# First linear map by 128-row blocks, the last four blocks' h kept on chip, y stored in 512-byte pieces

## The chip, the core and the metric

The kernel runs on one core of a Trainium2 chip. The metric is device time in microseconds (us), the median over runs of the same program. A profiled execution is one more run, with the hardware profiler on. Engines: PE is TensorE's matmul part and PEld its weight load, DVE is VectorE, ACT ScalarE, POOL GpSimd, SP SyncE, which here only issues DMAs. Each engine works through its own instructions in a fixed order; semaphores hold it where it needs another's result.

## The reference, cut to what matters

```python
# x: (8, 2048, 256); A: (2048, 2048), sparse, symmetric pattern; W1: (512, 256); W2: (256, 512)
A_norm = A + eye(n)
deg = sum(A_norm, axis=0) + sum(A_norm, axis=1) - diagonal(A_norm)
dinv = rsqrt(deg)
A_hat = A_norm * dinv[:, None] * dinv[None, :]
agg = einsum('nm,bmd->bnd', A_hat, x)
h = relu(batchnorm(agg.reshape(-1, 256) @ W1.T + b1))    # statistics over all 8 x 2048 rows
out = batchnorm(h @ W2.T + b2)
x1 = layernorm(x + out)
# then masked multi-head attention on x1 (4 heads of 64, mask where A is 0), residual and layernorm
```

Everything is float32. The change concerns the lines from `agg` to the product with `W2`. Both batch norms need all rows before the first normalised value exists, so they cut the program into stages.

## The kernel before

The 2048 rows are 16 blocks of 128, named t. Rows of all 8 batches stand side by side: a scaled x row is 8 x 256 = 2048 values, 8 KB, so one 128-row tile is 1 MB. Sixteen such tiles of chip memory, the "slots", are handed out by a small free list (class `Slot`), and every part of the first layer takes its large tiles from them.

*Dense stage* (lines 377 to 467). The adjacency rows are read and searched for their nonzeros; x is read in 1 KB rows, scaled by `dinv` and stored to `xs_d`; blocks 0 and 1, the dense ones, are summed over all of x with matmuls (L454).

*Sparse stage* (lines 469 to 628). For blocks 2 to 15 the neighbours of a row are listed, and a "tile" is one neighbour per row: GpSimd gathers 128 rows of `xs_d` by index (`gather`, L524, 1 MB) and beforehand the 128 adjacency values that go with them (L311). There are 116 tiles. A tile is added either by TensorE, as four 128x512 products with a one-hot or diagonal weight tile (L606), or by VectorE, as a multiply-add over 2048 columns (L593 for the first, L597 for the others). Blocks 2 and 3 have 14 and 11 tiles, of which 3 each are VectorE's; blocks 4 to 15 have 10 down to 6, of which 1 to 3 are TensorE's. VectorE also still searches the last adjacency rows (L219, L223, L226) during blocks 2 and 3. When a block's tiles are done, `add_rows` joins both sums (L355, four pieces, VectorE).

The gathers run ahead of their use. `gather_ahead` issues up to 8 tiles ahead, as long as more than `keep` slots are free; `keep` is 2, or 6 while the four turned tiles of the current four-block set have not yet been taken.

*First linear map.* `turn_rows` transposes a finished block (four transposes, one PSUM bank, one ACT copy L373; four times per block). The copies fill slots `agt[c, g]`: c is the set of four blocks (512 rows), g a pair of batches. So the four slots of a set are full when the fourth block is turned. Then `linear_steps(c, g)` computes h for two batches by 512 rows: for each 128 of the 512 outputs, two matmuls of 128x512 (four records in the trace, L489), one ACT copy with bias (L493), one `bn_stats` on VectorE (L476, issued one unit later). Call that a unit; there are 128. After four units an h tile of 1 MB is stored to `h_d` by SP (L496).

The order is written out by hand (`manual_schedule`). A list `work` holds generators; after each tile `do_work` takes one unit or one transposed quarter of it (two after a VectorE tile). Transposes go to the front of the list, linear units to its end: those of a set enter after its fourth block. What is left at the end of the tile loop is emitted in a row.

*Last loop and second linear map* (lines 636 to 792). The last four of the 32 h tiles are not stored. Their 16 units (L747) are interleaved with the finish of the first batch norm (`bn1.root`, `bn1.affine`) and with the ReLUs (L676) of the first two pairs of tiles. The other 28 tiles are read back (`read_h`), two per pair, up to 7 pairs ahead. For each pair `second_linear` makes the product with W2 by seven products of half size (Strassen's scheme; the differences of tiles are formed on GpSimd, L694, the products on TensorE, L699) and stores two y tiles of 512 KB to `y_d` (L729, L737), in rows of 4 KB. Then the second batch norm is finished and attention begins, whose first step loads y by batch and set of 512 rows (L870).

Of the kernel before, what the change touches and what calls it, by code (L numbers as in the profile page):

```python
# [8 lines left out]
F32 = mybir.dt.float32  # L9
# [4 lines left out]
AF = mybir.ActivationFunctionType  # L14
# [24 lines left out]
def tile_gcn_then_masked_attention(  # L39
# [15 lines left out]
    nc = tc.nc  # L55
    ENG = mybir.EngineType
    PSUM = bass.MemoryType.PSUM
    P = 128
# [276 lines left out]
    ps_a = None  # L335
    agr, agt = {}, {}

# [20 lines left out]

    def as_agt(s):
        return s.t.rearrange("p (d b n) -> p d b n", d=ND, b=2)  # L360

    def turn_rows(t, g, psum):

        c, i = divmod(t, TPC)
        if not i:
            agt[c, g] = Slot()
        ps = psum.tile([P, ND, 2, P], F32, name="ph")
        for d in range(ND):
            for b in range(2):
                r0 = (2 * g + b) * D + d * P  # L370
                nc.tensor.transpose(ps[:, d, b, :], agr[t].t[:, r0 : r0 + P], ident)
        dst = as_agt(agt[c, g])[:, :, :, i * P : (i + 1) * P]
        nc.scalar.copy(dst, ps)  # L373
        if g == B // 2 - 1:
            agr.pop(t).done()
# [93 lines left out]
    with tc.tile_pool(name="l0", bufs=1, side="right", reuse_waits="tile") as lp, tc.tile_pool(  # L469
        name="psh", bufs=4, space=PSUM  # L470
    ) as psh, tc.manual_schedule(engines=ALL4):
        last_stats = []

        def flush_stats():
            while last_stats:
                nc.vector.bn_stats(*last_stats.pop())  # L476

        def linear_steps(c, g):

            s = agt[c, g]  # L480
            v = as_agt(s)
            for b in range(2):
                k = (2 * g + b) * NCH + c
                h = lp.tile([P, NH, CH], F32, name="h", bufs=2)
                for f in range(NH):
                    flush_stats()
                    ph = psh.tile([P, CH], F32, name="ph")
                    for d in range(ND):
                        nc.tensor.matmul(  # L489
                            ph, w1s[:, d, f * P : (f + 1) * P], v[:, d, b, :],  # L490
                            start=(d == 0), stop=(d == ND - 1),
                        )
                    nc.scalar.activation(h[:, f, :], ph, AF.Identity, bias=b1s[:, f : f + 1])  # L493
                    last_stats.append((st1[:, f, k, :], h[:, f, :]))
                    if f == NH - 1:
                        nc.sync.dma_start(h_d[k], h)  # L496
                        if b:
                            s.done()
                    yield
# [29 lines left out]
        def gather_ahead(n):  # L529
            t = tiles[min(n, len(tiles) - 1)][0]  # L530
            keep = 2 if (t // TPC, B // 2 - 1) in agt else 2 + B // 2
            while gathered[0] < min(n + 8, len(tiles)) and (
                len(free) > keep or gathered[0] <= n
            ):
                gather(gathered[0])
                gathered[0] += 1
# [22 lines left out]
        def turn_steps(t):  # L559
            for g in range(B // 2):  # L560
                turn_rows(t, g, psh)
                yield

        for _ in turn_steps(0):
            pass
        work += [turn_steps(t) for t in range(1, DENSE)]
        gather_ahead(0)
# [3 lines left out]
        for n in range(len(tiles)):  # L571
# [40 lines left out]
            if n + 1 == first[t + 1]:  # L612
                add_rows(t, pa)
                do_work(2)
                work.insert(0, turn_steps(t))
                if t % TPC == TPC - 1 and t < NT - 1:
                    work += [linear_steps(t // TPC, g) for g in range(B // 2)]
            else:
                do_work(1 + mine)
        assert not making  # L620
        for f in work:
            for _ in f:
                pass
        for g in range(2):
            for _ in linear_steps(NCH - 1, g):
                pass
        flush_stats()
    right.close()
    middle.close()

    last4 = [b * NCH + NCH - 1 for b in range(B // 2, B)]
    others = [i for i in range(NALL) if i not in last4]
    pairs = [last4[:2], last4[2:]]
    pairs += [others[i : i + 2] for i in range(0, len(others), 2)]

    with tc.tile_pool(name="l1", bufs=1, side="right", reuse_waits="tile") as lp, tc.tile_pool(
        name="psa", bufs=4, space=PSUM
    ) as psa, tc.tile_pool(name="psh", bufs=4, space=PSUM) as psh, tc.manual_schedule(engines=ALL4):
        hin = {}

        def read_h(n):
            hin[n] = [Slot() for _ in range(2)]
            if n > 1:
                for r in range(2):
                    nc.sync.dma_start(hin[n][r].t, h_d[pairs[n][r]].rearrange("p f n -> p (f n)"))

        def h_tile(n, r):
            return hin[n][r].t.rearrange("p (f n) -> p f n", f=NH)

        w2s = [lp.tile([P, 2, O], F32, name=f"w2s{j}") for j in range(2)]  # L650
        w2f = [lp.tile([P, 2, P], F32, name=f"w2f{j}") for j in range(4)]
        for j in range(2):
            nc.sync.dma_start(
                w2s[j], w2t[j * 2 * P : (j + 1) * 2 * P].rearrange("(c p) f -> p c f", p=P)
            )
        for n in range(7):
            read_h(n)
# [45 lines left out]

        def first_product(n):
            Y[n] = [lp.tile([P, NO, CH], F32, name=f"y{n % 2}{r}") for r in range(2)]
            p1 = product2(W[0, 0], h_half(n, 0, 0))
            nc.scalar.copy(Y[n][0][:, 1, :], p1)
# [7 lines left out]
        def plus(dst, p, u, o):  # L715
            nc.vector.scalar_tensor_tensor(
                dst, p, b2s[:, o : o + 1], u, op0=ALU.add, op1=ALU.add
            )

        def second_linear(n):  # L720
            (c11, c21), (c12, c22) = ([Y[n][r][:, o, :] for o in range(NO)] for r in range(2))
# [6 lines left out]
            stats2(n, 1, 0)  # L728
            nc.sync.dma_start(y_d[pairs[n][0]], Y[n][0])  # L729
            if n not in P5:  # L730
# [5 lines left out]
            stats2(n, 0, 1)  # L736
            nc.sync.dma_start(y_d[pairs[n][1]], Y[n][1])  # L737
            for s in hin.pop(n):
# [3 lines left out]
        for f in range(NH):  # L742
            for n in range(B // 2):
                ph = psh.tile([P, CH], F32, name="ph")
                v = as_agt(agt[NCH - 1, B // 4 + n // 2])
                for d in range(ND):
                    nc.tensor.matmul(  # L747
                        ph, w1s[:, d, f * P : (f + 1) * P], v[:, d, n % 2, :],
                        start=(d == 0), stop=(d == ND - 1),
                    )  # L750
                h = h_tile(n // 2, n % 2)[:, f, :]
                nc.scalar.activation(h, ph, AF.Identity, bias=b1s[:, f : f + 1])
                nc.vector.bn_stats(st1[:, f, last4[n], :], h)
                if n == 0 and f:
                    bn1.affine(f - 1)
            bn1.root(f)
            if f:
                relu(0, f - 1)
                relu(1, f - 1)
            if f == 2:  # L760
                form(0, 1)
                form(1, 1)
        for g in range(B // 4, B // 2):
            agt[NCH - 1, g].done()
        bn1.affine(NH - 1)
        first_product(0)
        fifth_product(0, psh, "ph")
        first_product(1)
        fifth_product(1, psh, "ph")
# [4 lines left out]
        for n in range(len(pairs)):  # L774
            if n > 1:
                first_product(n)
            if 1 <= n < len(pairs) - 1:
# [4 lines left out]
            second_linear(n)  # L782
            if n + 7 < len(pairs):
                read_h(n + 7)

# [913 lines left out]
```

## Time and profile before

| | us |
|---|---|
| median of 3 runs | 2288.48 |
| lowest, highest | 2283.89, 2298.30 |
| profiled execution | 2305.59 |
| its span, first to last instruction | 2303.9 |

| stage, us from the span's start | length | PE busy | DVE busy | DMA share |
|---|---|---|---|---|
| dense, 0 to 185.4 | 185.4 | 149.4 | 141.5 | 0.80, then 0.84 |
| sparse and first linear, 185.4 to 583.5 | 398.1 | 360.1 | 360.9 | 0.90 |
| rest of the first linear, 583.5 to 663.2 | 79.7 | 76.8 | 37.2 | 0.53 |
| second linear, 663.2 to 845.5 | 182.3 | 180.5 | 118.4 | 0.52 |
| attention, 845.5 to 2303.9 | 1458.4 | 1233.4 | 1171.2 | 0.85 |

A stage's busy time is the time in which an engine had an instruction running; the difference to the stage's length is waiting. The DMA share is the mean busy share of the core's 16 DMA engines. The costliest groups around the change, from the page (line, engine, operation, out<-in, shape, count | busy us, mean ns of one | idle us just before them and what ended it):

```profile
L489 PE MATMUL ph<-e,w1s 128*128 128x512 f32 x448 | 197.4, 593 | 0.0
L524 POOL DMA_INDIRECT e<-xs_d,idx x116 | 152.9, 1318 | 138.9 <-DMA xs_d<-xt 66.6
L606 PE MATMUL pa<-e,wt 128*128 128x512 f32 x352 | 166.4, 621 | 14.6 <-DMA e<-xs_d,idx 11.2
L493 ACT ACTIVATE h<-ph,b1s 128x512 f32<-128x512 f32 x112 | 77.0, 687 | 179.9 <-PE ph L489 166.1
```

Matmuls are pipelined, so the 593 ns of one are longer than the distance from one to the next.

### The profile page before, as it was taken

Reading aid. Unit: us, or ns where it says so; the run is one execution under the profiler, and the core shown is the slowest. Engines: PE = TensorE matmul, PEld = TensorE weight load, DVE = VectorE, ACT = ScalarE, POOL = GpSimd, SP = SyncE. Lnnn points to the kernel's source line nnn. Section 1 sums busy time; section 2 is a strip of 40 time slices with the busy share of each in tenths; the row PEclk is TensorE's granted clock in tenths of the full one; section 3 lists DMA queues with packets and bytes.
Section 4 is the critical chain, followed back from the end, with each engine's and each line's share of the span. In section 5 each row is a group of like instructions: output and inputs, shape, how many; then the busy total and the mean of one; then the engine's idle time right before and its main releaser. Section 6 shows DMA issues by size and latency. Waiting matters only on the chain.

```text
span 2303.9 us, 27757 instructions
## 1 busy us (share of the span) xinstructions
PE 2000.2 (87%) x7720; PEld 1296.2 (56%) x7720; DVE 1829.2 (79%) x3461; ACT 1306.1 (57%) x3896; POOL 1443.2 (63%) x1443
## 2 busy tenths in 40 slices
PE   5899897898999979789889898989889999778774
PEld 1444443444444436566767766766667777556663
DVE  6888998798466652168799988889978999978896
ACT  6221132233355536556667776767767777678785
POOL 2505778884067741246667776667766777867784
PEclk7899998999999989989999999999999999889996
DMA  7888998899466445658889988789898899999994
GB/s 310 294 290 321 349 375 335 347 392 388 184 258 263 159 147 202 227 202 317 319 295 370 339 319 347 296 303 365 325 341 322 325 347 333 339 338 320 341 335 154
DMA packets 232628, 698.67 MB, mean 303 GB/s; under 512 B 24976, under 2 KB 91280, under 8 KB 206352
## 3 DMA queue, kind: packets, MB, share of 16 engines
q0 software_dynamic: 109248, 442.68, 52.1%
q1 hardware_dynamic: 120912, 237.34, 28.1%
q10 hardware_dynamic: 2304, 16.78, 1.8%
q8 instruction: 64, 1.05, 0.2%
q14 instruction: 100, 0.82, 0.1%
HBM read 565.91 MB, written 130.81 MB: 302 GB/s over the span
## 4 chain that ended last, share of the span: by engine, by line
PE 50%; DVE 23%; issue 7%; DMA 7%; ACT 5%; POOL 5%; another core or an unknown queue 1%; SPq 0%; DVEq 0%; ACTq 0%; POOLq 0%
PE po L1252 9%; PE pm L977 9%; PE pa L699 8%; PE ph L489 6%; DVE pr L1210 6%; PE pa L454 5%; DVE wv L1241 3%; DVE s L1212 3%; PE pa L606 3%; ACT wv L1236 2%; POOL kg L1192 2%; PE pm L1026 2%; PE po L1045 2%; DMA e<-in_adj_dram 2%; DMA e<-xs_d,idx 2%
## 5 line engine op out<-in xcount | busy, mean ns | idle before, releaser
L1192 POOL DMA_INDIRECT kg<-kv_d,idx x528 | 567.4, 1075 | 166.5 <-issue 102.9
L1252 PE MATMUL po<-wv,ident 128*128 128x260 f32 x1472 | 435.7, 407 | 96.5 <-DVE z L1066 85.6
L1236 ACT ACTIVATE wv<-kg,pw 128x65 f32<-128x65 f32 x1896 | 477.8, 338 | 21.3 <-issue 10.5
L1212 DVE TENSOR_REDUCE s<-pr 128x8 f32<-128x512 f32 x528 | 362.3, 686 | 34.4
L1252 PEld LDWEIGHTS po<-wv,ident 128*128 128x128 f32 x1472 | 278.5, 202 | 170.4 <-issue 107.9
L977 PE MATMUL pm<-wq,x1t 128*128 128x512 f32 (+1 forms) x1024 | 366.6, 489 | 1.0 <-ACT x1t L922 0.6
L1221 ACT ACTIVATE pw<-s,padb 128x8 f32<-128x8 f32 x528 | 156.6, 300 | 209.9 <-DVE s L1212 156.1
L1210 DVE TENSOR_TENSOR pr<-qb,kg 128x512 f32<-128x512 f32 x368 | 257.3, 699 | 5.0 <-DMA kg<-kv_d,idx 2.7
L1241 DVE TENSOR_TENSOR wv<-kg,pw 128x520 f32<-128x520 f32 x291 | 211.3, 726 | 58.7 <-PE po L1252 18.4
L977 PEld LDWEIGHTS pm<-wq,x1t 128*128 128x128 f32 x1024 | 193.8, 192 | 95.8 <-issue 74.1
L524 POOL DMA_INDIRECT e<-xs_d,idx x116 | 152.9, 1318 | 138.9 <-DMA xs_d<-xt 66.6
L1252 PE MATMUL po<-wv,oh 128*128 128x260 f32 x640 | 207.8, 415 | 0.3 <-DVE oh L1227 0.3
L489 PE MATMUL ph<-e,w1s 128*128 128x512 f32 x448 | 197.4, 593 | 0.0
L1198 POOL DMA_INDIRECT qg<-q_d,idxq x160 | 164.5, 1028 | 48.8 <-issue 47.8
L311 POOL DMA_INDIRECT av<-in_adj_dram,fidx x116 | 158.8, 1369 | 45.7 <-issue 32.3
L1026 PE MATMUL pm<-q,kt 128*128 128x256 f32 x512 | 141.9, 401 | 45.8 <-ACT kt L1014 19.1
L606 PE MATMUL pa<-e,wt 128*128 128x512 f32 x352 | 166.4, 621 | 14.6 <-DMA e<-xs_d,idx 11.2
L493 ACT ACTIVATE h<-ph,b1s 128x512 f32<-128x512 f32 x112 | 77.0, 687 | 179.9 <-PE ph L489 166.1
L1045 PEld LDWEIGHTS po<-kvr,p 128*128 128x128 f32 x1024 | 142.5, 203 | 22.9 <-ACT p L1034 11.4
L1073 POOL TENSOR_TENSOR x<-z,x 128x256 f32<-128x256 f32 x126 | 112.7, 896 | 57.1 <-DVE z L1066 52.5
L1045 PE MATMUL po<-kvr,p 128*128 128x65 f32 x1024 | 137.4, 280 | 11.5 <-ACT p L1034 8.9
L1026 PEld LDWEIGHTS pm<-q,kt 128*128 128x128 f32 x512 | 98.6, 199 | 84.3 <-ACT kt L1014 27.2
(192 smaller groups left out, 3399.0 us busy)
## 6 DMA issues: line engine op xcount, KB each, us to landing
kv_d<-kvr SPq DMA_DIRECT2D x32, 1032.0 KB
h_d<-h SPq DMA_DIRECT2D x28, 1024.0 KB
e<-h_d SPq DMA_DIRECT2D x28, 1024.0 KB
e<-in_adj_dram SPq DMA_DIRECT2D x16, 1024.0 KB
xt<-in_x_dram SPq DMA_DIRECT2D x16, 1024.0 KB
xs_d<-xt ACTq DMA_DIRECT2D x16, 1024.0 KB
y_d<-y SPq DMA_DIRECT2D x32, 512.0 KB
yt<-y_d SPq DMA_DIRECT2D x32, 512.0 KB
```

Source lines behind the costliest of these rows:

```text
L489: nc.tensor.matmul(ph, w1s[:, d, f * P : (f + 1) * P], v[:, d, b, :], start=(d == 0), stop=(d == ND - 1),)
L606: nc.tensor.matmul(pa[c], w, xg[n].t[:, c * CH : (c + 1) * CH], start=(k == 0), stop=(k == count - 1),)
L699: nc.tensor.matmul(py, w[:, f, :], t[:, f, :], start=(f == 0), stop=(f == 1))
L977: nc.tensor.matmul(pm, x1t[b, c][:, d, i * P : (i + 1) * P], rhs(d), start=(d == 0), stop=(d == ND - 1),)
L1026: nc.tensor.matmul(pm[:, hp].rearrange("p r q -> p (r q)"), k[:, hp, :], q0[b][:, hp].rearrange("p r q -> p (r q)"), start=False, stop=Tru ...
L1045: nc.tensor.matmul(po0[b][:, h, :], p[:, h, :], heads(kvr[b, c][:, i, D:])[:, h, :], start=(j == 0 and h == 0), stop=(j == NT - 1), skip_g ...
L1192: nc.gpsimd.indirect_dma_start(out=kg[n].rearrange("p b e -> p (b e)"), out_offset=None, in_=kv_d[p][:], in_offset=bass.IndirectOffsetOnAx ...
L1210: nc.vector.tensor_mul(pr, q, kg[n][:, :, :D])
L1212: nc.vector.tensor_reduce(s.rearrange("p b h -> p (b h)"), pr.rearrange("p b (h e) -> p (b h) e", e=HD), AX.X, ALU.add,)
L1236: nc.scalar.activation(wv[n][:, b, hs], k[:, b, D:][:, hs], AF.Copy, scale=w[:, b, h : h + 1],)
L1241: nc.vector.tensor_mul(wv[n].rearrange("p b (h e) -> p b h e", e=VW), k[:, :, D:].rearrange("p b (h e) -> p b h e", e=VW), w[:, :, :, None ...
L1252: nc.tensor.matmul(po[p, t, b].rearrange("p h e -> p (h e)"), oh[n] if e >= 0 else ident, wv[n][:, b, :], start=(r == 0), stop=(r == ELL[t ...
```

## The change

The set of the first linear map becomes "four batches by 128 rows" instead of "one batch by 512 rows". A block's transposes fill one slot `agb[t]` for all 8 batches, and `linear_steps(t)` can follow each block at once: two halves r (batches 0 to 3, 4 to 7), four units each. The number of units and the size of their matmuls are the same. An h tile is now block t, half r.

The units of blocks 0 and 1 are put on the work list before the tile loop, those of each later block after its transposes; only block 15's eight units stay for the last loop. The h tiles of blocks 12 to 15 (eight tiles, before four) stay in slots and are the first four pairs of the second linear map; 24 are stored and read back instead of 28, with reads up to 8 pairs ahead.

`gather_ahead` may be 10 tiles ahead instead of 8, and `keep` is now 2 plus `owed`, a count of slots that work already listed will still take (one for a turned block, two more for h that stays).

y keeps its layout in memory. As a pair of y tiles now holds four batches by 128 rows each, every tile is stored by four DMAs of 128 KB, in pieces of 512 bytes.

```diff
-    def as_agt(s):
-        return s.t.rearrange("p (d b n) -> p d b n", d=ND, b=2)
+    def as_agb(s):
+        return s.t.rearrange("p (d b n) -> p d b n", d=ND, b=B)
+
+    hin, owed, last_stats = {}, [0], []
+    LATE = NT - TPC
+    pairs = [(2 * t, 2 * t + 1) for t in (*range(LATE, NT), *range(LATE))]
...
+    def first_product(t, f, r, h, psum):
+
+        ph = psum.tile([P, CH], F32, name="ph")
+        for d in range(ND):
+            nc.tensor.matmul(
+                ph, w1s[:, d, f * P : (f + 1) * P],
+                as_agb(agb[t])[:, d, r * B // 2 : (r + 1) * B // 2, :],
+                start=(d == 0), stop=(d == ND - 1),
+            )
+        nc.scalar.activation(h[:, f, :], ph, AF.Identity, bias=b1s[:, f : f + 1])
+        last_stats.append((st1[:, f, 2 * t + r, :], h[:, f, :]))
 
     def turn_rows(t, g, psum):
 
-        c, i = divmod(t, TPC)
-        if not i:
-            agt[c, g] = Slot()
+        if not g:
+            agb[t] = Slot()
+            owed[0] -= 1
...
-        dst = as_agt(agt[c, g])[:, :, :, i * P : (i + 1) * P]
-        nc.scalar.copy(dst, ps)
+        nc.scalar.copy(as_agb(agb[t])[:, :, 2 * g : 2 * g + 2, :], ps)
...
-        def linear_steps(c, g):
-
-            s = agt[c, g]
-            v = as_agt(s)
-            for b in range(2):
-                k = (2 * g + b) * NCH + c
-                h = lp.tile([P, NH, CH], F32, name="h", bufs=2)
+        def linear_steps(t):
+
+            if t >= LATE:
+                hin[t - LATE] = [Slot() for _ in range(2)]
+                owed[0] -= 2
+            for r in range(2):
+                h = (
+                    h_tile(t - LATE, r) if t >= LATE
+                    else lp.tile([P, NH, CH], F32, name="h", bufs=2)
+                )
                 for f in range(NH):
                     flush_stats()
...
+                    first_product(t, f, r, h, psh)
                     if f == NH - 1:
-                        nc.sync.dma_start(h_d[k], h)
-                        if b:
-                            s.done()
+                        if t < LATE:
+                            nc.sync.dma_start(h_d[2 * t + r], h)
+                        if r:
+                            agb.pop(t).done()
                     yield
...
         def gather_ahead(n):
-            t = tiles[min(n, len(tiles) - 1)][0]
-            keep = 2 if (t // TPC, B // 2 - 1) in agt else 2 + B // 2
-            while gathered[0] < min(n + 8, len(tiles)) and (
+            keep = 2 + owed[0]
+            while gathered[0] < min(n + 10, len(tiles)) and (
                 len(free) > keep or gathered[0] <= n
             ):
...
+        owed[0] = DENSE
         for _ in turn_steps(0):
             pass
-        work += [turn_steps(t) for t in range(1, DENSE)]
+        work += [linear_steps(0)]
+        for t in range(1, DENSE):
+            work += [turn_steps(t), linear_steps(t)]
...
                 work.insert(0, turn_steps(t))
-                if t % TPC == TPC - 1 and t < NT - 1:
-                    work += [linear_steps(t // TPC, g) for g in range(B // 2)]
+                owed[0] += 1 if t < LATE else 3
+                if t < NT - 1:
+                    work.append(linear_steps(t))
...
-        for g in range(2):
-            for _ in linear_steps(NCH - 1, g):
-                pass
+        hin[NT - 1 - LATE] = [Slot() for _ in range(2)]
         flush_stats()
...
+        def store_y(n, r):
+            c, i = divmod(pairs[n][0] // 2, TPC)
+            for b in range(B // 2):
+                nc.sync.dma_start(
+                    y_d[(r * B // 2 + b) * NCH + c][:, :, i * P : (i + 1) * P],
+                    Y[n][r][:, :, b * P : (b + 1) * P],
+                )
...
-            nc.sync.dma_start(y_d[pairs[n][0]], Y[n][0])
+            store_y(n, 0)
...
-            nc.sync.dma_start(y_d[pairs[n][1]], Y[n][1])
+            store_y(n, 1)
...
         for f in range(NH):
-            for n in range(B // 2):
...
+            for r in range(2):
+                first_product(NT - 1, f, r, h_tile(NT - 1 - LATE, r), psh)
+                flush_stats()
+                if not r and f:
                     bn1.affine(f - 1)
             bn1.root(f)
             if f:
...
-            if n + 7 < len(pairs):
-                read_h(n + 7)
+            if n + 8 < len(pairs):
+                read_h(n + 8)
```

## What the change does to the time: a prediction

> **What bounds the kernel now.** I read the times first, then the page's slices and its groups, then the stretches between the borders of the stages and of the blocks, the chain of waits and the timeline of the part that the change touches. The median of three runs is 2288.48 us; the profiled execution took 2305.59 us (span 2303.9 and 1.7 around it), 0.75% more. I sum against the profiled execution and carry the difference over to the median.
>
> The stages, with busy time of PE, PEld, DVE, ACT and POOL, the granted clock, the DMA share and GB/s:
>
> ```profile
> 185.40:272.10 86.70, 76.94 (x229) 38.27 (x230) 85.69 (x136) 10.90 (x24) 59.62 (x50) 0.95 0.87 343
> 272.10:583.50 311.40, 283.18 (x823) 139.49 (x822) 275.19 (x526) 88.03 (x138) 221.80 (x154) 0.95 0.91 357
> 583.50:663.20 79.70, 76.79 (x190) 33.99 (x188) 37.19 (x59) 45.10 (x67) 17.80 (x18) 1.00 0.53 217
> 663.20:845.50 182.30, 180.47 (x420) 79.67 (x420) 118.42 (x175) 81.61 (x118) 138.36 (x59) 1.00 0.52 197
> ```
>
> Call the first row A (row blocks t = 2 and 3 of the sparse sum), the second B (t = 4 to 15), the third the tail, the fourth the second linear map. In A, VectorE is full (85.7 of 86.7) and TensorE has some 10 us free. In B both are near full, TensorE with 28 us free and VectorE with 36. In the tail TensorE alone is full. In the second linear map it is TensorE again, with DMA half idle. What lies behind 845.5 us is attention, whose instructions the change does not touch.
>
> Inside B the borders are the ends of L355, which closes each block. Blocks 4, 8 and 10, and the chain of waits (start us, us, what):
>
> ```profile
> 272.10:308.00 35.90, 35.16 (x99) 17.27 (x98) 35.46 (x62) 12.20 (x19) 25.82 (x19) 0.97 0.93 343
> 387.70:420.90 33.20, 28.41 (x79) 13.08 (x78) 25.99 (x65) 9.40 (x15) 27.41 (x20) 0.96 0.76 277
> 449.40:472.20 22.80, 22.80 (x71) 11.36 (x70) 21.78 (x49) 7.64 (x12) 18.32 (x13) 1.00 1.01 425
> ```
>
> ```profile
> 394.69 7.91 DMA e<-xs_d,idx
> ...
> 413.70 10.85 DMA e<-xs_d,idx
> ...
> 587.34 32.63 PE ph L489 x76
> 620.74 20.88 PE ph L747 x48
> ```
>
> Block 4 is as long as its VectorE work and block 10 as its TensorE work, so a block that isn't starved costs the larger of the two. Block 8 is starved: neither engine is full, DMA falls to 0.76, and the chain waits twice for a gathered tile. The last two lines are first-linear matmuls with nothing beside them that would need the time.
>
> **The change part by part.** *Units.* A unit is one 128x512 result of the first linear map: four matmul records. 76 records took 32.63 us, 0.429 us each, so 1.717 us a unit; it also costs one ACT copy (0.69) and one bn_stats on VectorE (0.69). There are 128 units before and after. What moves is where they stand, which the order of instructions of the two built programs shows. Before, A holds none, B 93, and 35 follow the last sparse product. After, A holds 24, B 92, and 12 follow.
>
> *A, dearer.* 24 units are 24 x 1.717 = 41.2 us of TensorE. Of its 76.9 busy us, 1.9 are transposes behind the last sparse product, so it needs 75 + 41.2 = 116.2, and with half a microsecond of the closing L355, 116.7. VectorE needs 85.7 + 24 x 0.69 = 102.3 and is hidden. A becomes TensorE-bound: 116.7 against 86.7, **+30**. VectorE's waits there (a bn_stats behind a late unit) hold up weights made three tiles ahead, so TensorE isn't held in turn; were it so, up to +38. If the queues interlock better than I count, +27.
>
> *B, cheaper.* By block I take VectorE's busy time less its L476 time, add eight bn_stats (5.5), and set it beside TensorE: 3.43 us a sparse product of four banks, 1.9 for 16 transposes, 0.9 for the list matmuls, 1.717 a unit. Blocks 4 to 15 give, as the larger one: 33.9, 26.8, 28.5, 25.3, 26.2, 25.1, 23.4, 23.4, 23.8, 22.4, 19.1, 19.1; sum 297. That needs the gathers to be in time. By the code's own count of slots, the old one is 3 to 6 tiles ahead in blocks 4 and 5, 8 and 9, and 12 and 13, because two sets of four turned tiles are held; there the waits above lie. The new one holds one turned tile a block and stays 10 ahead up to block 12, and falls to 7 only when h of blocks 12 to 14 takes six slots. On POOL's queue the gathers of adjacency values then no longer bunch four or five together between two row gathers. Its work is the same. Real blocks lie 0 to 1 us above the larger engine, so I take 301 for 311.4: **-10** (from -14 to 0).
>
> *Tail, cheaper.* 35 - 12 = 23 units leave it. The first 15 of them stand alone: 15 x 1.717 = **-25.8**. The other eight come out of the last loop, which interleaves the units with the first batch norm. That loop ran from 620.7 to the last ReLU's start at 654.4, 33.7 us. With two units a step, ACT sets its pace: 2 x 0.69 + 4 ReLUs of 0.73 = 4.3 us for three of four steps against 3.4 of TensorE. I count 19 us to the last h, 2.5 more for its statistics, root and scale: **-12** (from -9 to -14).
>
> *Queues and DMA.* h stores fall from 28 to 24 MB and so do the reads; on SP nothing else stands between the sweep's h stores, so the second weights and the reads start no later. Each 512 KB y store on SP becomes four of 128 KB with 512-byte pieces. The second linear map issues eight per pair of tiles instead of two, at about the 0.32 us of the old issue: 2.6 us of SP in 11.2 us of TensorE per pair. The next h read stands behind them, but it is eight pairs ahead. A 512-byte packet has no row. Nearest is the stage that loads x in 1 KB rows and stores 8 KB ones in equal bytes:
>
> ```profile
> 110.00:120.00 10.00, 10.00 (x25) 4.45 (x24) 9.90 (x6) 3.97 (x2) 0.00 (x0) 1.00 0.91 310
> ...
> 800.00:820.00 20.00, 20.00 (x48) 8.84 (x47) 13.05 (x20) 9.82 (x15) 15.95 (x7) 1.00 0.20 79
> ```
>
> The second row has y stores alone: 1 MB in 12 us at a share of 0.20 is 150 ns per 4 KB packet, 27 GB/s per engine. The first gives 21.3 GB/s per busy engine, so about 59 ns for 1 KB, 21 more than the bytes need. A 512-byte packet is then 19 + 21 = 40 ns. 32,768 of them are 82 us of 16 engines instead of 38; with 38 for 16 MB of h reads, 120 of 182 us. Hidden, **0**. Below, 19 ns a packet (bytes alone) is hidden too and can bring no gain, because TensorE is full; above, 86 ns is the average of the whole sync queue (28.1% of 16 x 2303.9 us over 120,912 packets), the rival below.
>
> Here the Trainium skill speaks against the change: "DMA: Bandwidth & Descriptors", "Anatomy of one DMA", gives a fixed 2.0 us per DMA plus the bytes at 436 GB/s, and its rules for authors ask for 1 MB or more. Eight stores of 2.3 us one behind the other are 18.4 us a pair, 16 pairs 294 us: about +112. By that same sum the old stores would take 6.4 of each 12 us, a share of 0.53. The trace has 0.20, so the fixed part is latency that overlaps, and I go with the row.
>
> *Start of attention.* The first y load (issued 845.46, landed 6.8 us later, ACT waiting) stands on SP behind four last stores instead of one, and their packets: **+2** (0 to +5). It needs chunk 0, long stored. Chunk 2 ends last, but its load is the third, 10 us later.
>
> Sum: +30 - 10 - 25.8 - 12 + 2 = **-16**. That makes 2290 for the profiled execution and 2288.5 - 16 = **2272** for the median.
>
> **The rivals.** *Larger gain.* Every bound at its good end: +27 - 14 - 25.8 - 14 + 0 = -27, so 2262. For it: blocks 4, 5, 10 and 11 run within 0.5 us of their larger engine today. Against: the new early blocks have no spare unit to fill a hole with.
>
> *No gain in B.* The sweep stays at 311 because DMA sets it. For it: the share is 0.91, and 1.01 in block 10. Against: 81 gathers and 18 h stores, about 104 MB, need 247 us at the 423 GB/s of that block. With A at +31, the tail -36 and +3 at attention: -2, so 2286.
>
> *Slower: the y stores bind the second linear map.* At 86 ns a packet they need 176 us, with the reads 214 against 182: +31. TensorE would then wait for h reads behind the stores, and the sum is +15: 2304. It decides from (182 - 38) x 16 / 32,768 = 70 ns. Against it stand the 59 ns of twice the size.
>
> **How the numbers follow.** Forecast 0.55, larger gain 0.20, no gain in B 0.14, slower 0.11. One per cent is 23 us, about what this kernel's runs can tell from nothing. The larger gain lies mostly beyond it, and so does a good quarter of the forecast's own range (-28 to -5): faster 0.34. Slower by over 1% is most of the last rival, 0.08. The rest, 0.58, is within 1%; as faster and same hold nearly all, the forecast's own range is 2260 to 2284. The wide range is 2253 to 2298: it takes in the larger gain, no gain in B, and the y stores up to 82 ns a packet.
>
> **What would show it.** First-linear matmuls (L489 before) between the sparse products (L606) from 190 us on; block 3 closing near 302 us instead of 272; block 15 near 603 instead of 583.5; 42 us instead of 79.7 from there to the steady second linear map; still 182 us from that to attention, at a DMA share near 0.7; no wait for a row gather over 5 us in B. The forecast is wrong if A grows by under 20 or over 40 us, if blocks of B exceed their larger engine by over 3 us, or if the DMA share of the second linear map passes 0.9 and TensorE waits there for h.

## The result, and the profile after

The changed kernel took 2270.05 us, the median of 6 runs (2264.55 to 2278.39), against 2289.57 us for the kernel before (6 runs). The ratio is 0.9914, 95% interval 0.9886 to 0.9943: 19.5 us less, between 13 and 26. The prediction was 2272 us, its forecast -16. On a second chip the same two kernels lie 14.5 us apart (2236.16 and 2221.70). The profiled execution after is the run of 2278.39 us; its span is 2276.7.

The stretches between the same borders as before (busy time of PE, PEld, DVE, ACT, POOL; granted clock, DMA share, GB/s), in the profile after. In order: A (row blocks 2 and 3), B (blocks 4 to 15), the rest up to the steady second linear map, the second linear map, attention:

```profile
185.20:299.00 113.80, 113.80 (x316) 54.34 (x317) 99.43 (x158) 25.35 (x46) 50.94 (x47) 1.00 0.86 333
299.00:600.10 301.10, 280.53 (x827) 138.84 (x826) 275.50 (x526) 88.42 (x139) 225.83 (x153) 0.97 0.91 347
600.10:644.30 44.20, 38.78 (x97) 17.21 (x96) 20.74 (x34) 29.27 (x44) 18.04 (x18) 0.96 0.46 190
644.30:829.10 184.80, 180.45 (x421) 79.61 (x419) 120.81 (x179) 81.62 (x118) 139.51 (x63) 1.00 0.58 183
829.10:2276.70 1447.60, 1230.49 (x5622) 937.71 (x5622) 1167.25 (x2414) 1008.25 (x3464) 953.58 (x1095) 0.94 0.85 310
```

In the first row TensorE is busy for the whole 113.8 us: A has changed its bound, from VectorE to TensorE. The third row has lost 35.5 us against before, the second 10.3, and the first has gained 27.1. With +2.5 in the fourth, the stages that the change touches give 27.1 - 10.3 - 35.5 + 2.5 = -16.2 us. The attention row, 1458.4 before and 1447.6 here, is the rest; its instructions are the same.

TensorE's timeline at the head of A, after (start, duration, instruction, count of records):

```profile
186.96 3.60 PE L621 MATMUL pa<-e,wt 128*128 128x512 f32 x8
190.40 1.88 PE L377 MATMUL ph<-e,w1s 128*128 128x512 f32 x4
192.12 3.60 PE L621 MATMUL pa<-e,wt 128*128 128x512 f32 x8
195.55 1.88 PE L377 MATMUL ph<-e,w1s 128*128 128x512 f32 x4
```

L621 is the sparse product and L377 the first linear map (L606 and L489 before). A sparse product is eight records. One unit, four records, stands behind each, with no gap.

Two more views need both kernels. First the waits of TensorE in B, before (what it waited for: us in total, times, longest):

```profile
PE ph L371 <- DVE e L355: 12.8, 3, 4.8
PE pa L606 <- DMA e<-xs_d,idx: 11.2, 4, 5.9
PE ph L272 <- DVE oh L265: 3.3, 1, 3.3
```

The same view after:

```profile
PE ph L394 <- DVE e L355: 16.3, 4, 5.5
PE ph L254 <- DVE junk L243: 2.3, 1, 2.3
PE ph L254 <- ACT e L395: 1.0, 1, 1.0
```

The waits for a gathered tile are gone. The waits of the transposes (L371 before, L394 after) for the block's last sum are still there and longer. What that says comes out of the experiments.

The chain of waits after, from B on, where it names a gather or the second linear map (start, us, what):

```profile
365.67 8.55 DMA e<-xs_d,idx
381.00 7.63 DMA e<-xs_d,idx
402.95 10.07 DMA e<-xs_d,idx
...
639.26 183.78 PE pa L702 x424
829.06 5.59 DMA yt<-y_d
```

Gathers are still on the chain in blocks 6 to 8, through other engines than TensorE. The second linear map is one step from end to end: its products wait for nothing.

### The profile page after: what moved, and what is told of

Read it like the earlier page. It is cut to its first block, busy times and chain, and to the rows that moved or that the text cites. A ratio compares the mean times of both kernels' runs of the same rounds, so it can differ in the third digit from the quotient of the medians.

```text
span 2276.7 us, 27878 instructions
## 1 busy us (share of the span) xinstructions
PE 1990.9 (87%) x7720; PEld 1291.8 (57%) x7720; DVE 1825.2 (80%) x3461; ACT 1305.8 (57%) x3896; POOL 1440.1 (63%) x1443
## 4 chain that ended last, share of the span: by engine, by line
PE 54%; DVE 20%; issue 8%; ACT 6%; DMA 5%; POOL 5%; another core or an unknown queue 1%; SPq 0%; DVEq 0%; ACTq 0%; POOLq 0%
PE po L1255 10%; PE pm L980 9%; PE pa L702 8%; PE ph L377 7%; PE pa L621 6%; DVE pr L1213 5%; PE pa L476 5%; DVE wv L1244 3%; ACT wv L1239 3%; DVE s L1215 3%; PE po L1048 2%; PE pm L1029 2%; POOL kg L1195 2%; DMA e<-in_adj_dram 2%; DVE ln_st L836 1%
## 5 line engine op out<-in xcount | busy, mean ns | idle before, releaser
L1215 DVE TENSOR_REDUCE s<-pr 128x8 f32<-128x512 f32 x528 | 362.1, 686 | 35.5 <-ACT wv L1239 0.5
L377 PE MATMUL ph<-e,w1s 128*128 128x512 f32 x512 | 228.0, 593 | 0.8 <-ACT e L382 0.8
L382 ACT ACTIVATE h<-ph,b1s 128x512 f32<-128x512 f32 x96 | 66.0, 688 | 195.7 <-PE ph L377 182.1
L621 PE MATMUL pa<-e,wt 128*128 128x512 f32 x352 | 164.7, 612 | 0.0
L377 PEld LDWEIGHTS ph<-e,w1s 128*128 128x128 f32 x512 | 95.9, 190 | 115.4 <-issue 112.4
```

The costliest lines, as they stand in the source:

```text
L377: nc.tensor.matmul(ph, w1s[:, d, f * P : (f + 1) * P], as_agb(agb[t])[:, d, r * B // 2 : (r + 1) * B // 2, :], start=(d == 0), stop=(d == ...
L621: nc.tensor.matmul(pa[c], w, xg[n].t[:, c * CH : (c + 1) * CH], start=(k == 0), stop=(k == count - 1),)
L1215: nc.vector.tensor_reduce(s.rearrange("p b h -> p (b h)"), pr.rearrange("p b (h e) -> p (b h) e", e=HD), AX.X, ALU.add,)
```

## The experiments

Ten kernels ran: y_split, ahead_4, late_16 and before_again on one chip, the other six on a second one. Each ratio is to the kernel before, run on the same chip beside it (2304.99 us on the first, 2236.16 and later 2238.14 on the second); medians from different chips are not to be compared. The table gives the stage lengths of one profile each. "Rest" is the first linear map behind block 15's sum up to the steady second linear map, and "second" runs from there to attention's first load of y; the border between the two is read to some 0.5 us.

| kernel | A | B | rest | second | median us | ratio to before, interval |
|---|---|---|---|---|---|---|
| before | 86.7 | 311.4 | 79.7 | 182.3 | 2289.57 | |
| before_again | 86.7 | 308.1 | 79.6 | 182.3 | 2300.57 | one run |
| y_split | 86.7 | 312.2 | 79.6 | 184.8 | 2304.79 | 0.9999, 0.9985 to 1.0013 |
| after | 113.8 | 301.1 | 44.2 | 184.8 | 2270.05 | 0.9914, 0.9886 to 0.9943 |
| after_again | 113.8 | 299.1 | 45.3 | 185.2 | 2221.70 | 0.9934, 0.9921 to 0.9948 |
| ahead_4 | 113.8 | 302.5 | 43.9 | 185.2 | 2289.43 | 0.9942, 0.9921 to 0.9964 |
| old_gathers | 113.8 | 301.5 | 44.0 | 185.2 | 2222.91 | 0.9948, 0.9933 to 0.9964 |
| store_h | 113.8 | 301.2 | 47.2 | 184.8 | 2224.23 | 0.9943, 0.9928 to 0.9959 |
| late_16 | 98.7 | 304.2 | 45.3 | 185.6 | 2275.93 | 0.9893, 0.9872 to 0.9913 |
| late_16_again | 98.7 | 304.1 | 45.2 | 185.1 | 2213.98 | 0.9898, 0.9882 to 0.9913 |
| sets_of_4 | 86.7 | 305.0 | 83.6 | 185.1 | 2238.41 | 0.9999, 0.9989 to 1.0009 |
| late_24 | 86.7 | 302.6 | 56.0 | 185.1 | 2211.54 | 0.9884, 0.9866 to 0.9901 |

Up to the y stores y_split is the kernel before, so three profiles show the old B: 308.1, 311.4 and 312.2 us. The changed one is 299.1 and 301.1. So B is read to 2 to 4 us.

**y_split: the y stores alone.** The kernel before, with each of its y stores cut into four.

```diff
+        def store_y(n, r):
+            for i in range(TPC):
+                at = slice(i * P, (i + 1) * P)
+                nc.sync.dma_start(y_d[pairs[n][r]][:, :, at], Y[n][r][:, :, at])
...
-            nc.sync.dma_start(y_d[pairs[n][0]], Y[n][0])
+            store_y(n, 0)
...
-            nc.sync.dma_start(y_d[pairs[n][1]], Y[n][1])
+            store_y(n, 1)
```

> The kernel before, with one thing changed: each 512 KB y store is four DMAs of 128 KB in pieces of 512 bytes. My theory (40 ns a packet, hidden behind TensorE): the second linear map stays at 182 us (within 2), its DMA share rises from 0.52 to about 0.65, attention starts 1 to 3 us later, the time is 0 to +4 us of the kernel before. Rival one (86 ns a packet): +15 to +31 us and TensorE waits for h reads. Rival two (2.3 us of fixed cost each, one after the other): over +100 us.

The ratio is 0.9999. The second linear map, from its steady part to attention's first load of y, and a stretch of it in which only y is stored, in the profile of y_split:

```profile
664.60:849.35 184.75, 180.51 (x420) 79.71 (x420) 120.62 (x179) 81.59 (x118) 139.71 (x63) 1.00 0.61 195
800.00:820.00 20.00, 20.00 (x48) 8.82 (x47) 12.44 (x18) 11.26 (x17) 14.74 (x8) 1.00 0.27 76
```

The second row answers to the one at 800 us in the prediction, which had a share of 0.20 at 79 GB/s. With y alone in it, 16 engines busy for 0.27 of the time at 76 GB/s make 0.27 x 16 x 512 / 76 = 29 ns per 512-byte packet; by the same sum the old 4 KB packet took 166 (the prediction had 150). TensorE is full in both. The stores are dearer for the DMA engines than before, but hidden behind TensorE, and the stage is 2.5 us longer. Where those lie can be seen on SP's queue in the changed kernel, at the end of the stage:

```profile
825.69 2.61 SPq L726 DMA_DIRECT2D y_d<-y  x4
828.41 0.60 SPq L805 DMA_DIRECT2D bias<-bias_d  x1
829.06 0.45 SPq L873 DMA_DIRECT2D yt<-y_d  x1
```

The last tile's four stores (L726) take 2.61 us to issue ahead of attention's first load of y (L873). That is 0.65 us each, twice the 0.32 us that the prediction took from the old large store: some 5 us of SP for a pair of tiles instead of 2.6, still less than the 11.4 us that a pair takes.

**before_again: the profile of before once more**, on y_split's chip.

> The kernel before, once more, for how much the length of attention (from the first load of y to the end) changes from one profiled execution to the next. In the two profiles at hand it was 1458.4 us before and 1447.6 after, though its instructions are the same. If that is chance, this run differs from 1458.4 by several us too; if the change shortened it, this run shows 1455 to 1461.

B is 308.1 us and attention 1456.3. Alone, that would speak for a shorter attention by the change; the other profiles speak against it. Attention is 1458.4 and 1447.6 in the two profiles of the main comparison, and on y_split's chip 1450.0 in y_split (old units), 1456.4 in ahead_4 (new units) and 1449.7 in late_16, with the same instructions throughout. On the second chip all six kernels have 1390.3 to 1394.6. So the 10.8 us by which attention is shorter after lie within what unchanged work varies by.

**ahead_4: short distance of the gathers.** The prediction's reason for B was that the new kernel's gathers run further ahead.

```diff
-            while gathered[0] < min(n + 10, len(tiles)) and (
+            while gathered[0] < min(n + 4, len(tiles)) and (
```

> The changed kernel, with the gathers at most 4 tiles ahead instead of 10. If the sweep over blocks 4 to 15 got shorter (311 to 301 us) because gathers are no longer late, it gets longer again here: 311 to 330 us, with TensorE and VectorE waiting for row gathers of over 5 us, and the time is +10 to +30 us of the changed kernel (about even with the kernel before). The rival, that the way the units are spread made the sweep shorter and the distance of the gathers doesn't matter, expects 301 us and no change against the changed kernel (ratio to the kernel before near 0.991).

B is 302.5 us, within the spread of 299.1 and 301.1. Blocks 8, 9 and 13 take 29.8, 24.9 and 23.1 us, as in the changed kernel, and neither TensorE nor VectorE waits for a gather in B. With units after every block, four tiles ahead are enough.

**old_gathers: the gathers of before in their old order.** The same from the other side: a table (`GATHERED`, its numbers left out here) says how many gathers have been issued before each tile, as it was in the kernel before with its pauses and bursts.

```diff
-            keep = 2 + owed[0]
-            while gathered[0] < min(n + 10, len(tiles)) and (
-                len(free) > keep or gathered[0] <= n
-            ):
+            while gathered[0] < GATHERED[min(n, len(tiles) - 1)]:
```

> The changed kernel with its units as they are, but every row gather issued after the same tile as in the kernel before, so that GpSimd's order is that of the kernel before (pauses of four to five tiles, then several at once). Theory A, that not the distance but these pauses made blocks 8, 9 and 13 of the kernel before late: they take about 33, 28 and 27 to 29 us again instead of 29.9, 24.8 and 23.1, blocks 4 to 15 together 308 to 313 us, the time +6 to +12 us of the changed kernel. Theory B, that the spread of the units alone did it: 301 us, no change against the changed kernel.

B is 301.5 us, and blocks 8, 9 and 13 take 30.9, 25.2 and 23.0 instead of 33, 28 and 27 to 29. The order of the gathers alone does not bring the old time back either.

**after_again: the changed kernel on the second chip**, the base for its neighbours.

> The changed kernel once more, beside the three runs that follow, on one chip. Ratio to the kernel before 0.989 to 0.994 as in the first comparison; stages as in its first profile within 1 us (blocks 2 and 3: 113.8, blocks 4 to 15: 301, tail 44), attention anywhere from 1446 to 1460.

The ratio, 0.9934, lies inside the interval of the first comparison, and the stages agree to 2 us. Attention, at 1394.4, lies far below what was expected; so it does in all profiles of this chip.

**store_h: h of blocks 12 to 14 stored and read back**, so that only block 15's stays.

```diff
-    LATE = NT - TPC
+    LATE = NT - 1
...
-        for n in range(TPC, TPC + 3):
+        for n in range(1, 7):
...
-        read_h(TPC + 3)
+        read_h(7)
```

> The changed kernel, but h of blocks 12 to 14 is stored and read back like the others; only block 15's two tiles stay on chip (30 MB each way instead of 24). If keeping four blocks has no part in the gain, as I reckoned: blocks 4 to 15 301 to 304 us, tail 44 to 47, second linear map 185, the time 0 to +4 us of the changed kernel. If the DMA traffic of h is what the sweep or the tail waits for: +8 to +15 us, with TensorE waiting for h stores or reads.

Against after_again the rest takes 47.2 us for 45.3 and the whole 2224.23 for 2221.70; the intervals overlap. What keeping four blocks on chip is worth, some 2 us by these figures, can't be told from nothing.

**late_16: units of blocks 1 and 2 held until block 4.** A has only about 10 us of TensorE free, so 24 units there cost 27. Held, 16 of them go to B, where TensorE has 20 us free.

```diff
+        held = []
         for t in range(1, DENSE):
-            work += [turn_steps(t), linear_steps(t)]
+            work += [turn_steps(t)]
+            held.append(linear_steps(t))
...
-                if t < NT - 1:
+                if t == DENSE:
+                    held.append(linear_steps(t))
+                elif t == DENSE + 1:
+                    work += [*held, linear_steps(t)]
+                elif t < NT - 1:
                     work.append(linear_steps(t))
```

> The changed kernel, with the 16 units of blocks 1 and 2 held back until block 4, so that only block 0's eight stand in the first part of the sweep. My theory (blocks 2 and 3 are bound by TensorE's extra units, blocks 4 to 9 by VectorE with TensorE to spare): blocks 2 and 3 take about 91 to 94 us instead of 113.6, blocks 4 to 15 about 309 to 313 instead of 301 (16 more bn_stats of 0.69 us), the tail the same 44: 9 to 14 us faster than the changed kernel, ratio to the kernel before about 0.986. The rival, that the sweep is bound as a whole by TensorE's total, expects the 23 us to come back in blocks 4 to 15: no change against the changed kernel.

A falls by 15.1 us, B grows by 3.1 (301.1 to 304.2), so the sum falls by 12.0. B stayed below what was expected of it, with TensorE busy for 300.2 us of it, and A above: eight units, 13.7 us of TensorE's work, cost 12 us there although some 10 us were free. The waits in A of late_16 say why:

```profile
PE ph L394 <- DVE e L355: 8.1, 1, 8.1
DVE st L371 <- ACT h L382: 7.5, 5, 2.8
```

VectorE, the fuller engine, loses 7.5 us behind the units' copies, and TensorE then waits 8.1 us for VectorE to close block 3. The free time lay at the end of the stretch, the units at its head.

**late_16_again: the same on the second chip**, beside after_again.

> The version with 16 units held back until block 4, beside the changed kernel on the same chip. By the stages of its first profile (98.7, 304.2 and 45.3 against 113.8, 301.1 and 44.0) it is 10.7 us faster than the changed kernel, ratio to the kernel before about 0.987; if the stages mislead and attention takes it back, no difference to the changed kernel.

It took 2213.98 us against 2221.70 for the changed kernel there, 7.7 us less for an expected 10.7; the intervals don't overlap. A, B and rest repeat to 0.1 us.

**sets_of_4: the changed kernel with the units in sets again.** The layout by 128 rows, the slots and the four blocks of h stay; `owed` counts one slot instead of three for a late block, and what is held at the end follows the loop.

```diff
-        work += [linear_steps(0)]
+        held = [linear_steps(0)]
         for t in range(1, DENSE):
-            work += [turn_steps(t), linear_steps(t)]
+            work += [turn_steps(t)]
+            held.append(linear_steps(t))
...
-                owed[0] += 1 if t < LATE else 3
+                owed[0] += 1
                 if t < NT - 1:
-                    work.append(linear_steps(t))
+                    held.append(linear_steps(t))
+                if t % TPC == TPC - 1 and t < NT - 1:
+                    work += held
+                    held = []
...
-        for f in work:
+        for f in [*work, *held]:
```

> The changed kernel, with the units of four blocks put on the work list together after the set's fourth block, as the kernel before has them; the layout by 128 rows, the slots, the four blocks' h on chip and the y stores stay as changed. The units of blocks 12 to 14 stand at the end. Theory B (what the sparse blocks 4 to 15 gained comes from spreading the units over all blocks, none of it from layout, slots or distance of the gathers): A 86.8 us, B 308 to 312 with block 7 below 23 us and block 13 above 26, the rest of the first linear map 44 + 23 x 1.717 = 83.5 us, the second linear map 185; together some 5 us more than the kernel before, ratio 1.000 to 1.004. Rival (the layout or the slots gave it): B 301 to 304, so 2 to 4 us less than the kernel before, ratio 0.997 to 0.999, and block 13 at 23 us.

The stretches A, B and rest of sets_of_4:

```profile
185.80:272.50 86.70, 75.09 (x229) 37.87 (x230) 85.69 (x137) 10.80 (x24) 56.92 (x46) 0.96 0.90 359
272.50:577.50 305.00, 281.41 (x823) 138.53 (x822) 274.59 (x524) 87.97 (x138) 226.14 (x155) 0.96 0.93 358
577.50:661.10 83.60, 78.18 (x189) 34.30 (x188) 36.74 (x58) 45.07 (x67) 17.87 (x18) 0.98 0.35 132
```

A and the rest came out as expected, and the whole gain is gone (0.9999): it is the units' place. B, however, fell between the two theories, at 305.0 in this one profile: 3 to 7 us below the three of the old B, 4 to 6 above the changed kernel's. The waits of its TensorE in B, and one of its VectorE's:

```profile
PE ph L394 <- DVE e L355: 12.4, 5, 4.8
PE ph L272 <- DVE oh L265: 9.4, 1, 9.4
PE pa L622 <- DMA e<-xs_d,idx: 1.0, 1, 1.0
DVE wgt L323 <- DMA av<-in_adj_dram,fidx: 10.6, 3, 5.8
```

TensorE's waits for gathers, 11.2 us in before, 6.9 in before_again and 4.2 in y_split, are down to 1.0 with the units still in sets. But VectorE waits 10.6 us there for gathered adjacency values (L323), where the old kernel's three profiles have 3.2 to 4.6. The longest of these waits, 5.84 us, ends in block 7 at 382.20, 4.4 us before TensorE's 9.4 us wait for VectorE (L265) does. With both engines' waits for gathered rows and values added, the old B has 23.1, 20.7 and 18.1 us, sets_of_4 has 14.6, the changed kernel 0.4 and none, ahead_4 and old_gathers none. So in these profiles the gathers are late where the units stand in sets, and in time where they are spread; the new gathers and slots seem only to soften it. Block 13 shows TensorE's side of it. Its timeline there, before (a bracket is the idle time ahead of the instruction and what ended it):

```profile
520.71 3.60 PE L489 MATMUL ph<-e,w1s 128*128 128x512 f32 x8
530.23 5.28 PE L606 MATMUL pa<-e,wt 128*128 128x512 f32 x8 [5.92 <-DMA e<-xs_d,idx]
```

GpSimd's timeline a little later, before:

```profile
538.48 0.94 POOL L524 DMA_INDIRECT e<-xs_d,idx  x1 [0.30 <-issue]
546.61 0.94 POOL L524 DMA_INDIRECT e<-xs_d,idx  x1 [7.19 <-DVE e L597]
```

TensorE waits 5.92 us for a gathered tile. Later GpSimd stands still for 7.19 us until VectorE gives a slot back; that is one of the old pauses, but it comes behind the wait and didn't cause it. Block 13 took 29.1 us (27.0 in before_again), 22.1 in sets_of_4 and 23.1 in the changed kernel. Block 7, expected below 23 us by the first theory, took 26.2. The first theory had both blocks wrong; the rival, which named block 13 alone, had that one.

**late_24: all 24 units of A held until block 4.** late_16 with its first line changed to hold block 0's units as well.

```diff
-        work += [linear_steps(0)]
+        held = [linear_steps(0)]
         for t in range(1, DENSE):
-            work += [turn_steps(t), linear_steps(t)]
+            work += [turn_steps(t)]
+            held.append(linear_steps(t))
```

> The changed kernel with all 24 units of blocks 0 to 2 held until block 4. Theory (A is VectorE's with some 10 us of TensorE free, and B in the version that held 16 units was already TensorE's from end to end): A falls to 86.8 us, B takes eight units more, 304 + 8 x 1.717 = 318 us, and the sum A + B is 405, 2 us more than with 16 held; ratio to the kernel before 0.989 to 0.992. Rival (B has room left): B stays at 304 to 310, and the whole is 6 to 12 us shorter than with 16 held, ratio 0.984 to 0.987.

The stretches A, B and rest of late_24:

```profile
186.20:272.90 86.70, 76.75 (x229) 38.40 (x230) 85.70 (x137) 10.80 (x24) 56.55 (x46) 0.95 0.89 354
272.90:575.50 302.60, 300.51 (x887) 147.24 (x886) 283.72 (x540) 98.28 (x154) 225.44 (x155) 1.00 0.94 370
575.50:631.50 56.00, 50.59 (x125) 22.36 (x124) 25.64 (x42) 34.08 (x51) 17.76 (x18) 0.97 0.40 152
```

TensorE is busy for 300.5 of B's 302.6 us. B did not take the eight more units that the expectation gave it: the list gives out about one unit a tile, so seven went on to the rest, which grew from 45.2 to 56.0. Altogether 2.7 us less than late_16_again in these three stretches (445.3 against 448.0) and 2.4 in the medians, whose intervals overlap. Both held versions beat the changed kernel; which of the two is better isn't told.

The three stretches together, with PE's busy time out of the same windows, give one account for all versions. What TensorE does is the same, 1240 to 1242 records; what differs most is how long it stands still:

| kernel | A + B + rest | PE busy | PE idle |
|---|---|---|---|
| before | 477.8 | 436.9 | 40.9 |
| sets_of_4 | 475.3 | 434.7 | 40.6 |
| after | 459.1 | 433.1 | 26.0 |
| late_16 | 448.2 | 429.0 | 19.3 |
| late_24 | 445.3 | 427.9 | 17.4 |

Of the 32.5 us between the first and the last row 23.5 are idle time. The other 9.0 are busy time, though the records are the same in number. A long wait costs more than its length, as a short wait in block 7 of before and the long one in its block 13 show:

```profile
373.07 3.67 PE L606 MATMUL pa<-e,wt 128*128 128x512 f32 x8 [0.70 <-DMA e<-xs_d,idx]
530.20:532.70 2.50, 2.47 (x3) 1.16 (x4) 0.18 (x1) 0.00 (x0) 1.89 (x3) 0.50 0.93 299
```

Behind 0.70 us of waiting a sparse product takes 3.67 us, as elsewhere. Behind 5.92 us it took 5.28, and the second line has the granted clock over its first 2.5 us: 0.50, against 1.00 over 520.70 to 524.30, ahead of the wait. The first sparse product behind a wait of 2.6 to 5.9 us takes 4.4 to 5.4 us in the profiles of before and after. That all 9 us come from this was not tested.

In the changed kernel 20.6 of the 26.0 lie in B (301.1 - 280.5), and 16.3 us of waiting there are transposes held by the block's last sum: TensorE's own queue has no unit left to put in between. In late_16, with spare units on the list, that wait is down to 3.0, and in late_24 TensorE's only wait in B is this:

```profile
PE ph L394 <- DVE e L355: 1.3, 1, 1.3
```

## Why the prediction was right

*A, +30.* Measured +27.1. TensorE became the bound, as said, and is busy for the whole stretch. The term was 3 us too large, at the good end of its bounds. The sum carried over 75 us of the old stretch's busy time, and that was taken with waits in it, at a granted clock of 0.95; the new stretch has neither waits nor a lower clock (113.8 of 113.8 busy, 1.00). That VectorE's waits would hold up the weights did not happen.

*B, -10.* Measured -10.3 in the first pair of profiles, -9.0 in the second (308.1 to 299.1). The size was right, the starving was real, and the reason given for its end was wrong. The step said that the blocks are starved because the old gathers are 3 to 6 tiles ahead and bunched, and that the new ones stay 10 ahead. With units after every block, 4 ahead (302.5) and the old gather order (301.5) are as good, and neither TensorE nor VectorE waits for gathers there. With units in sets, the new gathers and slots go with about half of the difference (305.0, one profile), and VectorE still waits for gathered values. It is the spread of the units that ends the starving. Why it does was not measured; which part of "gathers and slots" softens it, with units in sets, wasn't separated.

That the sum came out so well is in part luck. The reckoning had each block 0 to 1 us above its larger engine, and called itself wrong if blocks exceed it by over 3 us. Block 8, after:

```profile
418.22:448.10 29.88, 25.12 (x71) 12.44 (x70) 26.07 (x67) 7.65 (x12) 24.70 (x18) 0.90 0.97 363
```

It took 29.9 us with VectorE, its larger engine, busy for 26.1: 3.8 above, so by that sign the reckoning by blocks failed. Block 14 took 15.4 for the 19.1 reckoned and cancels it. Part of the apparent starving was also only moved: block 7, with no unit listed, ran through in 21.7 us before, and blocks 8 and 9 then paid. The three together took 83.4 us before, 82.3 after and 79.2 in sets_of_4.

*Tail, -25.8 and -12.* Measured 79.7 to 44.2, -35.5. The 15 units that stood alone are gone; the last loop gave about 10 instead of 12, inside its bounds. The timeline of VectorE, ScalarE and GpSimd at its end, after:

```profile
626.59 4.66 POOL L697 TENSOR_TENSOR x<-e,e 128x1024 f32<-128x1024 f32 x2
...
628.98 2.27 DVE L159 TENSOR_TENSOR rs<-mv,sc 128x1 f32<-128x1 f32 x1
...
631.49 2.93 ACT L679 ACTIVATE e<-e,sh,sc 128x512 f32<-128x512 f32 x4 [3.38 <-DVE sh L160]
```

The norm's scale for one quarter (L159, one value per row) took 2.27 us here and 0.16 at 623.65. It ends at 631.25, when the second of GpSimd's two differences of tiles (L697) does. ScalarE then waited 3.38 us for the shift (L160). The step counted 2.5 us for statistics, root and scale, without GpSimd's work beside them; that this made the 2 us was not tested.

*y stores, 0.* Right, by y_split. The estimate of 40 ns a packet was too high: 29, and a DMA share of 0.58 to 0.61 instead of near 0.7. Four small stores in place of one leave the time unchanged (0.9999, 0.9985 to 1.0013), so the +112 us of the serial sum fall. The rule behind that sum ("DMA: Bandwidth & Descriptors", "Anatomy of one DMA", in the Trainium skill: a fixed 2.0 us a DMA) is given there for DMAs that GpSimd issues, and these stores are SP's. Adding it up over DMAs one behind the other was the prediction's reading of it. The slower rival, 86 ns a packet and +31, falls too.

*Start of attention, +2.* Measured +2.5, and +2.5 in y_split, which has nothing of the change but the stores.

*The rivals.* "No gain in B, DMA sets it" falls with B's 301.1 us. More than that, at 0.94 of DMA share late_24 puts seven per cent more matmul records through B than the changed kernel did (887 for 827) in 302.6 us against 301.1. "Larger gain" named what speaks against it, no spare unit to fill a hole with, and this was the point: with spare units in B (late_16) the further gain came. (The 423 GB/s taken for block 10 are block 11's; block 10 has 425. It changes nothing.)

The stages sum to -16.2 for a forecast of -16. The median's -19.5 is 3 us further and the second chip's -14.5 is 2 short, both well within the interval of -13 to -26.

## What to carry to other kernels

Before filler work is spread evenly, set each stage's busy times beside its length and put the filler only where its engine has holes. Here, 24 units brought forward into a stage with 10 us of room cost 27 us, and holding most or all of them back for the next stages won 8 to 10 us on top of the change (2221.70 to 2213.98 and 2211.54). Add busy and idle time of the bounding engine over all the stages that share the work: that sum told what a version had gained, while single blocks mostly traded time with each other.

## What the runs showed of the hardware

The same program differed by 3% between two chips: the kernel before took 2304.99 us on one and 2236.16 on the other, medians of 24 and 9 runs. For late_16, profiled on both, the difference is attention (1449.7 against 1394.6 us), while A, B and rest agree to 0.1 us each. Each chip was used once, so it isn't told whether the chip or the hour made it.

Small stores were cheap: a packet of 512 bytes took 29 ns of a DMA engine, one of 4 KB 166. Eight small packets thus cost 1.4 times the large one. SP took 0.65 us to issue a small store and 0.32 for a large one.

A sparse product behind a wait of 5.92 us took TensorE 5.28 us instead of 3.60, at a granted clock of 0.50 over the first 2.5 us. So that wait cost 1.7 us on top of its idle time.

A VectorE instruction on one value per row took 2.27 us instead of 0.16 while GpSimd worked on 128x1024 tiles, and ended with GpSimd's instruction. It took 2.27 us in the old kernel's profiles too. That GpSimd was the cause was not tried.
